# Moving the extra bank half's sum behind the last pair's matmuls, and one factor copy ahead of V0's and V1's copies

## The chip, the cores and the metric

The kernel runs on one core of a Trainium2 chip. The metric is the device time of one execution in microseconds (us). The kernel before was run three times: 461.73, 462.26 and 461.80 us, median 461.80 us.

## What is computed

The reference is a compressed interaction network of three layers over x of shape 1024 x 64 x 16 (batch, feature, embedding):

```python
h = x
for i in range(3):
    z = einsum('bfe,bge->bfge', x, h).reshape(B, 64 * fh, 16)
    y = einsum('oc,bce->boe', W[i], z) + b[i]        # 128 channels
    x_i, h = (y[:, :64], y[:, 64:]) if i < 2 else (y, y)
    xs.append(x_i)
out = sum(concatenate(xs, 1), axis=2) @ fc_w.T + fc_b  # (1024, 1)
```

Everything is float32. The output is one number per batch row, so the part of each layer that goes only into the sum can be folded into weights. The kernel does that: V0 and V1 are such folded weights (`v0`, and `va`/`vb`, made from `in_wx`), and the third layer is folded with `fc_w` into one quadratic form whose matrix lies in `md`.

## The kernel before, in words

**Tiles.** The batch is cut into 32 chunks of 32 rows; a chunk has N = 32 x 16 = 512 columns. For a chunk, `xa` holds the features in four rotations (128 x 4 x 512) and each quarter `xb[j]` holds one further rotation (128 x 512). A product block z is `xa` times one quarter, 128 x 2048, made by VectorE (DVE) or GpSimd (POOL). Before DVE multiplies, ScalarE (ACT) copies the quarter into a PSUM bank (`second`, L550 to L553; the pool tag "y" has two such banks). Sixteen 128-row slices of z against `w_all` give a layer.

**Pairs.** Most chunks go in pairs. A pair's two chunks are multiplied together with fewer matmuls by mixing their z blocks first (`w_mix`, L640 to L652, on POOL: T2 from T3 and X, T3 from T3 and B22, T2 from T2 and B21) and using sums and differences of weights (`ws`). A pair has PSUM banks `alpha`, `delta` and `beta`. Each matmul is 128 rows by 64 columns of weights, so it uses one half of the array's columns and writes one half of a bank; `window` and `zipped` write the matmuls of the two halves alternately into TensorE's (PE's) queue. `squares` then adds terms in x squared and V0 times x (64 x 64 matmuls, four at once).

**Order.** All of this is written by hand: `at(when, fn, ...)` collects steps, and at the end they are emitted in order of `when` (ties in order of collection). So `when` is a place in the queues, not a time. Each engine works through its own queue in that order.

**The first pair (k = 3, chunks 6 and 7).** `make_pair` (L687) emits its copies and products. The product of chunk 6 with quarter 1 is the first pair's X of j = 1; it stands at 26, and its copy `second` at 26 - 2.7 = 23.3. Earlier stand the steps that make V0 and V1: `weigh` on POOL (4 and 5), `add_up` on DVE (17 and 20, L539) and `place` on ACT (17.1 and 20.1, L544). So on ACT the order is: V0's copies, V1's copies, then the copy of chunk 6's quarter 1.

**The end.** The last pair is k = 15. After its window, from t on, two columns are zipped together: the first (one array half) holds three `beta` jobs, two `gamma` jobs (`left_run` with `gamma`), three `delta` jobs and then `end_q` for chunk 3; the second (the other half) holds three `end_q` of chunk 2, seven `alpha` jobs, one `alpha` job with `vb`, and then `end_q` of chunk 2. `gamma` is the half of alpha's bank that alpha leaves free. Its content belongs to alpha's sum: `end_gamma` (L940 to L943), at t + 5, copies it on ACT to the partitions of alpha (L942) and adds it there on DVE into the alpha bank (L943). Chunks 2 and 3 were started at the head of the kernel and end here: `end_squares` at t + 10.5 makes `hx` and `y` (four 64 x 64 matmuls), adds `hx` to the kept `hb` on DVE (L930) and copies two quadrants of it on ACT (L932). `end_pair` emits the last pair's DVE steps: `w_hb` (L665), `w_qa` (L669), `w_ha` (L672), `w_uu` for the second chunk (L675), `x_v0x` (L288, which reads the pair's y bank), and at 13.8 `w_uu` for alpha (L675) and at 14.5 the sum (L292). Then come `x_v0x` and the sum of chunks 2 and 3, `add_parts` (L951), the q sum's second part (34 matmuls of 128 columns), the pooling matmuls (`pools`) and the output.

Of the kernel before, what the change touches and what calls it, by code (L numbers as in the profile page):

```python
# [68 lines left out]
def cin_kernel(ctx, tc, xra, xrb, wh, w0r, w1h, w2t, wx1, wx0, vec, out):  # L69
# [297 lines left out]
    for h in range(2):  # L367
        at = slice(32 * h, 32 * h + 32)
# [145 lines left out]
    def at(when, fn, *args, **flags):  # L514
        ops.append((when, len(ops), fn, args, flags))
# [163 lines left out]
    def make_pair(t, p, when, mixed):  # L679
        a, b = p["a"], p["b"]  # L680
        for when, c, j, name, uses in (
            (when[0], b, 2, "B22", 5), (when[1], b, 0, None, 0), (when[2], b, 0, "T3", 9),
            (when[3], a, 0, "X", 5), (when[4], b, 3, "B22", 6), (when[5], b, 1, None, 0),
            (when[6], b, 1, "T3", 9), (when[7], a, 1, "X", 12 if p["k"] > 3 else 6), (when[8], a, 2, "B21", 5),
            (when[9], a, 3, "B21", 6),
        ):
            if name is None:  # L687
                at(t + when, w_both, p, j)
                continue
            if name == "B21" and j == 2 and p["k"] == 3:  # L690
                at(t + when, w_product, p, c, j, name, uses, engine=nc.gpsimd)
                continue
            if name != "T3":
                at(t + when - (3.3 if p["k"] > 4 and name == "B22" and j == 2 else 2.7), second, c, j)
            at(t + when, w_product, p, c, j, name, uses)
        for when, j, *names in zip(
            mixed, (0, 1, 0, 1, 0, 1), *zip(
                *(2 * (("T2", "T3", "X"),) + 2 * (("T3", "B22", "T2"),) + 2 * (("T2", "T2", "B21"),))
            )
        ):  # L700
            at(t + when, w_mix, p, j, *names)
# [42 lines left out]
    def end_pair(t, p, whens):  # L744
        hb_, qa, uub, ha, uua, xv, add = whens
        at(t + hb_, w_hb, p)
        at(t + qa, w_qa, p)
        at(t + uub, w_uu, p, alpha, "A", snaps[2])
        at(t + ha, w_ha, p)
        at(t + uua, w_uu, p, delta, "O", snaps[0])  # L750
        at(t + xv, x_v0x, p["k"])
        at(t + add, sums, p["k"])
# [80 lines left out]
    for n in range(NPAIR):  # L833
        k = n + 3
        s = k % 2
        p = {
            "k": k, "A": halves[s], "O": halves[1 - s], "b": 2 * k + s, "a": 2 * k + 1 - s,
            "late": 1 + n % 2 if n else 0,
        }
        pairs.append(p)  # L840
        t = T0 + SPAN * n
        if n == 0:
            load_pair(t, p, -39.9, -33.3, -33.15, -27)
            make_pair(
                t, p, (-23.4, -20.7, -20.4, -17.8, -17.2, -16.8, -16.6, -7, -13.5, 3),
                (-14, -6.9, 7.2, 12.4, 16.4, 21.7),
            )
            left5 = [[(contract_half, 5, 3, i, n) for i in (2, 3)] for n in range(2)]
            window(
                t, p, ([left5[1][0], (q_extra, 4, va)], [left5[1][1]]),  # L850
                [left5[0][0], (q_extra, 5, va), None, None], [left5[0][1], None],
                GROUPS,
            )
        else:
            q = pairs[-2]
            load_pair(t, p, -34, -28, -27.8, -27.7)
            make_pair(
                t, p, (-21.4, -18.7, -18.4, -15.8, -12.2, -9.5, -6.1, -2, 1.6, 4.2),
                (-5, 2.8, 7.2, 12.4, 16.4, 21.7),
            )  # L860
            window(t, p, (first_fill(q), second_fill(q)), late_run(q))
            end_pair(t, q, (0.7, 11.7, 17.9, 22.3, 23.2, 24, 27.5))
# [40 lines left out]
    t, q = T0 + SPAN * NPAIR, pairs[-1]  # L903
# [65 lines left out]
    for when, c in ((-5, 2), (0, 3)):  # L969
        at(t + when, product, c, NJ - 1, engine=nc.gpsimd, uses=NI)  # L970
    end_pair(t, q, (0.7, 4.5, 13.8, 8.5, 9, 9.5, 14.5))
    at(t + 5, end_gamma)
    at(t - 0.1, new_ends)
    zipped(
        t,
# [2 lines left out]
        [(end_q, 2, m, 0) for m in range(3)] + late_run(q, False)  # L978
        + [(end_q, 2, m, 0) for m in range(3, NT)] + [(end_extra, 2, 0)],
    )  # L980
    at(t + 10.5, end_squares)
    at(t + 15, x_v0x, 1)
    at(t + 15.1, sums, 1, of=slice(1, 2))
    t += 25
# [98 lines left out]
```

## Time and profile before

| what | value |
|---|---|
| median of three runs | 461.80 us |
| the profiled execution, whole | 462.24 us |
| its span in the trace | 460.4 us |
| PE busy | 453.5 us, 99% |
| DVE busy | 394.0 us, 86% |
| POOL busy | 367.7 us, 80% |
| ACT busy | 117.1 us, 25% |
| TensorE clock granted | 1.00 |

The span is the part that the trace covers; the whole execution has 1.84 us around it. One float32 matmul shows as two records of about 0.59 us. Records of one array half follow one another at 0.43 us (512 columns), the two halves run side by side, and so PE counts as busy as long as one of the halves works. Times within the trace are us from the start of the span. A line of the timeline has start, duration, engine, line of the code, operation, out<-in, how many were merged, and in brackets the idle time before and what ended it.

### The profile page before, as it was taken

The numbers are of one execution on the slowest core, as the hardware profiler recorded it, in microseconds if no ns is written. First come the engines' busy times: TensorE is split into PE (matmuls) and PEld (weight loads), VectorE is DVE, ScalarE is ACT, GpSimd is POOL, SyncE is SP. The second block draws the span as 40 slices with busy tenths as digits, with TensorE's granted clock in tenths as the row PEclk, the third lists the DMA queues.
The fourth block names the chain that finished last, engine by engine and source line by source line (L and its number), as shares of the span: only waits on it lengthen the run. The fifth ranks groups of instructions, "written<-read, shape, count | busy, mean of one in ns | idle before, by whom it ended". The sixth has DMA issues, their size and how long they took to land.

```text
span 460.4 us, 6106 instructions
## 1 busy us (share of the span) xinstructions
PE 453.5 (99%) x2328; PEld 166.5 (36%) x2328; DVE 394.0 (86%) x284; ACT 117.1 (25%) x216; POOL 367.7 (80%) x112
## 2 busy tenths in 40 slices
PE   7999999999999999999999999999999999999997
PEld 4565343343333333333333333333333333333335
DVE  3995599899898989989898998989899998979551
ACT  2162250241313123131213213131311313124011
POOL 5323688998998979899798979989798989989800
DMA  8996998393728173663818264481827448240000
GB/s 295 417 297 149 324 407 321 130 323 111 270 86 319 30 260 140 188 212 131 282 35 290 100 233 166 135 277 48 304 73 250 161 163 279 79 149 18 22 0 2
DMA packets 32613, 86.04 MB, mean 187 GB/s; under 512 B 6116, under 2 KB 6788, under 8 KB 27656
## 3 DMA queue, kind: packets, MB, share of 16 engines
q1 hardware_dynamic: 31800, 84.70, 53.4%
q10 hardware_dynamic: 784, 0.95, 0.8%
q8 instruction: 18, 0.29, 0.3%
q14 instruction: 11, 0.09, 0.1%
HBM read 84.00 MB, written 1.64 MB: 186 GB/s over the span
## 4 chain that ended last, share of the span: by engine, by line
PE 82%; DMA 7%; DVE 3%; SPq 2%; POOL 2%; ACT 1%; issue 1%; POOLq 0%; DVEq 0%
PE alpha L524 57%; PE delta L524 9%; PE beta L524 7%; PE q L524 3%; DMA z<-in_wx 3%; PE acc L250 2%; DMA xa<-in_xra 2%; DVE z L632 2%; DMA xb<-in_xrb 1%; DMA md<-z 1%; SPq L457 1%; POOL z L240 1%; POOL z L535 1%; PE misc L113 1%; PE xp L219 1%
## 5 line engine op out<-in xcount | busy, mean ns | idle before, releaser
L647 POOL TENSOR_TENSOR z<-z,z 128x2048 f32<-128x2048 f32 x78 | 310.4, 4019 | 31.3 <-PE alpha L524 31.3
L632 DVE TENSOR_TENSOR z<-xa,xp 128x2048 f32<-128x2048 f32 x103 | 232.6, 2280 | 16.2 <-POOL z L647 13.1
L524 PE MATMUL alpha<-z,ws 128*64 128x512 f32 x624 | 211.6, 592 | 0.6 <-DVE alpha L943 0.6
L524 PE MATMUL delta<-z,ws 128*64 128x512 f32 x364 | 163.1, 594 | 0.0
L524 PEld LDWEIGHTS alpha<-z,ws 128*64 128x64 f32 x624 | 66.4, 137 | 113.5 <-issue 110.7
L524 PE MATMUL beta<-z,w_all 128*64 128x512 f32 x234 | 105.0, 593 | 0.0
L552 ACT COPY xp<-xb 128x512 f32<-128x512 f32 x88 | 51.6, 588 | 204.8 <-DVE z L632 181.3
L524 PE MATMUL alpha<-z,w_all 128*64 128x512 f32 x208 | 94.2, 595 | 1.1 <-DVE uu L288 0.7
L524 PEld LDWEIGHTS delta<-z,ws 128*64 128x64 f32 x364 | 48.6, 137 | 13.6 <-issue 11.2
L240 DVE TENSOR_TENSOR z<-xa,xp 128x2048 f32<-128x2048 f32 (+2 forms) x23 | 45.1, 2003 | 9.6 <-ACT xp L552 8.2
L524 PEld LDWEIGHTS alpha<-z,w_all 128*64 128x64 f32 x208 | 27.4, 137 | 61.1 <-issue 48.0
L240 POOL TENSOR_TENSOR z<-xa,xb 128x2048 f32<-128x2048 f32 x6 | 27.2, 4557 | 20.6 <-DMA xb<-in_xrb 20.6
L524 PEld LDWEIGHTS beta<-z,w_all 128*64 128x64 f32 x234 | 31.4, 137 | 14.6 <-issue 14.5
L250 PE MATMUL acc<-z,w_all 128*64 128x256 f32 x256 | 29.1, 382 | 1.6 <-DVE z L240 1.4
L524 PE MATMUL acc<-z,w_all 128*64 128x512 f32 (+1 forms) x96 | 30.0, 594 | 0.0
L524 PE MATMUL delta<-z,w_all 128*64 128x512 f32 x52 | 24.6, 593 | 0.0
L250 PEld LDWEIGHTS acc<-z,w_all 128*64 128x64 f32 x256 | 18.0, 137 | 13.8 <-DVE z L240 3.1
L292 DVE TENSOR_REDUCE acc<-uu 128x64 f32<-128x1024 f32 (+2 forms) x19 | 19.6, 1035 | 0.2
L638 DVE TENSOR_TENSOR xp<-xp,xb 128x512 f32<-128x512 f32 x26 | 18.2, 699 | 0.8
L655 ACT COPY snap<-alpha 64x512 f32<-64x512 f32 x13 | 7.6, 581 | 41.7 <-PE delta L524 34.2
L524 PE MATMUL y<-e,v 64*64 64x512 f32 x64 | 17.0, 613 | 0.0
L524 PE MATMUL q<-z,w_all 128*64 128x384 f32 (+1 forms) x128 | 16.9, 381 | 0.0
(117 smaller groups left out, 322.5 us busy)
## 6 DMA issues: line engine op xcount, KB each, us to landing
xa<-in_xra SPq DMA_DIRECT2D x32, 1024.0 KB, 4.7
xb<-in_xrb SPq DMA_DIRECT2D x128, 256.0 KB, 6.8
e<-in_xra SPq DMA_DIRECT2D x28, 128.0 KB, 4.5
xx<-in_xra SPq DMA_DIRECT2D x28, 128.0 KB, 2.5
z<-in_w2t SPq DMA_DIRECT2D x2, 1024.0 KB
z<-in_wx SPq DMA_DIRECT2D x2, 1024.0 KB, 9.2
z<-in_w1h SPq DMA_DIRECT2D x1, 1024.0 KB
xa<-in_xra SPq DMA_DIRECT2D x3, 256.0 KB
```

The source lines that it names most:

```text
L113: nc.tensor.matmul(misc[:, 0:n], zeros, zeros[:, 0:n], start=True, stop=True)
L219: nc.tensor.matmul(xbs[c][j][halves[h]], shift[halves[r], at : at + F], xas[c][halves[r], 0, :], start=True, stop=True,)
L240: engine.tensor_tensor(blocks[zs[c, j]][:, at, :], xas[c][:, at, :], xbs[c][j].unsqueeze(1).to_broadcast([128, last - first, N]), ALU.mult,)
L250: nc.tensor.matmul(accs[c][halves[n]], w_all[:, t, 0:64], blocks[zs[c, j]][:, i, n * H2 : (n + 1) * H2], start=(t == 0), stop=(j == last a ...
L292: nc.vector.tensor_reduce(acc[rows, of, k, half], uu[rows, of if at is None else at, E * half.start : E * half.stop].rearrange("p k (b e) ...
L457: queue.dma_start(out=ms[halves[half], 1, j * NI : (j + 1) * NI], in_=skewed(0, 16 * half + 4 * (j + 1), [[row, NI], [1, F]]),)
L524: nc.tensor.matmul(out, w, rhs, start=start, stop=stop, skip_group_check=True)
L552: nc.scalar.copy(bank, xbs[c][j])
L632: engine.tensor_tensor(blocks[b], xas[c], xbs[c][j].unsqueeze(1).to_broadcast([128, NI, N]), ALU.mult)
L638: nc.vector.tensor_tensor(bank, bank, xbs[p["b"]][j], ALU.add)
L647: nc.gpsimd.tensor_tensor(blocks[o][:, tiles], blocks[x][:, tiles], blocks[y][:, tiles], ALU.subtract)
L655: nc.scalar.copy(snaps[0][p["O"]], alpha(p))
```

## The change

Three places in the emission order are changed. The copy of the first pair's X factor of j = 1 moves from 23.3 to 26 - 9.1 = 16.9, ahead of `place` for V0 (17.1) and V1 (20.1). `end_gamma` moves from t + 5 to t + 11.6. `end_squares` moves from t + 10.5 to t + 10.9. No instruction is added or taken away.

```diff
@@ -691,7 +691,10 @@
                 at(t + when, w_product, p, c, j, name, uses, engine=nc.gpsimd)
                 continue
             if name != "T3":
-                at(t + when - (3.3 if p["k"] > 4 and name == "B22" and j == 2 else 2.7), second, c, j)
+                ahead = 3.3 if p["k"] > 4 and name == "B22" and j == 2 else 2.7
+                if p["k"] == 3 and name == "X" and j == 1:
+                    ahead = 9.1
+                at(t + when - ahead, second, c, j)
             at(t + when, w_product, p, c, j, name, uses)
@@ -969,7 +972,7 @@
     end_pair(t, q, (0.7, 4.5, 13.8, 8.5, 9, 9.5, 14.5))
-    at(t + 5, end_gamma)
+    at(t + 11.6, end_gamma)
     at(t - 0.1, new_ends)
@@ -978,7 +981,7 @@
-    at(t + 10.5, end_squares)
+    at(t + 10.9, end_squares)
     at(t + 15, x_v0x, 1)
```

Seen engine by engine, PE, POOL and the DMA queue keep their order. On ACT the one copy stands ahead of V0's copies instead of behind V1's, and the copy of gamma stands behind the two quadrant copies of L932 instead of ahead of them. On DVE the gamma add stands behind the `hb` add of L930, just ahead of alpha's `w_uu`, instead of ahead of `w_ha`.

## The prediction

> **What bounds the kernel now.** I read the engine shares first (PE 99% of the span), then the chain of waits, then the two stretches that the change touches. PE bounds nearly everywhere, so an edit pays only where PE, or one half of its array, stands. The chain leaves PE in a few places; two are concerned. The first, from the chain in order of time (start us, us, what):
>
> ```profile
> 80.14 2.30 DVE shift L539
> ...
> 83.44 0.60 ACT xp L552
> 84.04 0.02 issue
> 84.07 2.29 DVE z L632
> 86.36 0.67 DVE uu L288
> 87.03 0.04 issue
> 87.07 1.07 PE alpha L524 x2
> ```
>
> V1's reduction, V1's four small copies on ACT (82.46 to 83.43, left out here), the factor copy behind them, the first pair's X product, one more DVE step, and then the first pair's first matmul. The copy waits for nothing but its place in ACT's queue. What stands later in that pair shows in the weight loads of PE, timeline (in brackets the idle time of the load path and what ended it):
>
> ```profile
> 105.01 0.13 PEld L524 LDWEIGHTS delta<-z,ws 128*64 128x64 f32 x1 [0.39 <-POOL z L647]
> ...
> 108.42 0.13 PEld L524 LDWEIGHTS delta<-z,ws 128*64 128x64 f32 x1 [0.37 <-POOL z L647]
> ...
> 112.36 0.13 PEld L524 LDWEIGHTS alpha<-z,w_all 128*64 128x64 f32 x1 [0.99 <-DVE z L632]
> ```
>
> Delta's last seven jobs wait for POOL's mixes, and the next pair's first job waits for DVE. The second stretch is the end. PE timeline:
>
> ```profile
> 432.91 0.59 PE L524 MATMUL alpha<-z,ws 128*64 128x512 f32 x1
> 433.11 0.59 PE L524 MATMUL beta<-e,va 128*64 128x512 f32 x1
> 433.33 2.08 PE L524 MATMUL alpha<-z,ws 128*64 128x512 f32 x7
> 435.26 1.02 PE L524 MATMUL delta<-z,w_all 128*64 128x512 f32 x2
> 436.85 0.64 PE L524 MATMUL alpha<-z,ws 128*64 128x512 f32 x1 [0.57 <-DVE alpha L943]
> ...
> 441.19 1.02 PE L524 MATMUL alpha<-e,vb 128*64 128x512 f32 x2
> 442.14 0.64 PE L524 MATMUL hx<-e,vs 64*64 64x512 f32 x1
> ```
>
> The third alpha job waits for the gamma add on DVE, which waits for the gamma copy on ACT. The idle column says 0.57 us, because one half still works on delta until 436.12; the alpha half has stood since 434.62. DVE's side of it, timeline:
>
> ```profile
> 436.08 0.71 DVE L943 TENSOR_TENSOR alpha<-alpha,snap 64x512 f32<-64x512 f32 x1 [1.66 <-ACT snap L942]
> 438.83 0.69 DVE L672 TENSOR_TENSOR delta<-delta,snap 64x512 f32<-64x512 f32 x1 [2.04 <-PE delta L524]
> 439.56 0.68 DVE L675 SCALAR_TENSOR_TENSOR uu<-delta,snap 64x512 f32<-64x512 f32 x1
> 440.17 0.73 DVE L288 SCALAR_TENSOR_TENSOR uu<-y,cx,xx 128x512 f32<-128x512 f32 x1
> ```
>
> **What the Trainium skill says.** "TensorEngine Tiling (Array Packing)", Key Properties: tiles operate independently, and a change of tiling mode drains TensorE. The trace agrees: the halves carry streams of their own, and the change to 64 x 64 tiles costs 0.09 us (the last alpha slot ends at 441.62 + 0.43 = 442.05, hx starts at 442.14). "TensorE: Matmul & The Clock Gate", Part 3, The mechanism, says matmuls start and end in strict queue order. Across halves this trace differs: the first alpha job (432.91) starts ahead of the gamma job that stands before it in the queue (433.54, when beta's half is free). One unstarted matmul of the other half can be passed; I go by the trace. "Perfetto Trace Analysis", Per-instruction lifecycle, says that waits and the spreading of semaphores lie outside the profiled windows; here that tail is 0.06 us (L943 ends at 436.79, alpha starts at 436.85).
>
> **The change, part by part: the end.** Removed from PE's path: the wait of the third alpha job. ACT's 0.58 us and DVE's 0.71 us are not saved, they move. I lay out both halves from 432.91 with 0.857 us for a 512-column job (two records at 0.43) and 0.645 us for a 384-column q job (two at 0.32).
> - Alpha half: jobs 1 and 2 from 432.91 to 434.62, then six more without a wait: 434.62 + 6 x 0.857 = 439.77.
> - Other half: gamma from 433.54, two gamma and three delta jobs, three q jobs: 433.54 + 5 x 0.857 + 3 x 0.645 = 439.77.
> Both end together, where before the alpha half ended at 442.05: 2.28 us less. Then hx can start at 439.77 + 0.09 = 439.86.
>
> What is late next: the y matmul behind the first hx overwrites the bank that L288 reads. Before, L288 ended at 440.90 and hx started at 442.14, so that wait was covered. Now L672 starts when delta is done. Before, it started 1.07 us after the last delta job's start (437.76 to 438.83); now that job starts at 433.54 + 4 x 0.857 = 436.97, so L672 starts at 438.04, L288 at 439.38, and ends at 440.11. With 0.06 us, y starts at 440.17, 0.30 us after hx. Behind it in PE's queue stand the second hx, the second y and all remaining q matmuls. From the squares to the first q behind them it takes 1.02 us (442.14 to 443.16), so q starts at 440.17 + 1.02 = 441.19 instead of 443.16: **1.97 us**. The bounds: 1.64 if the halves keep strict order (the third alpha job then starts with delta at 435.27 and the half ends at 440.41, so hx and y at 440.50 and q at 441.52), and 2.28 if the y wait costs nothing.
>
> hx itself now carries waits for DVE and ACT of its own: its bank was read last by L669 (ended 434.42) and its input e was made by ACT squares before 424.2, so they cost nothing.
>
> The moved sum: L930 follows hx (second hx about 440.2, its second record ends near 441.3), to 442.0; two quadrant copies on ACT 1.25, to 443.3; gamma copy 0.58, to 443.9; then DVE: add 0.71, L675 0.69, L292 1.22, L288 0.75, L292 0.69, L951 0.72, to about 448.9 with gaps. Before, L951 ended at 448.15. Who waits: the pooling matmuls at 454.30 before, now 452.33, and the q factor step at 452.54 before, now 450.6. About 3.4 and 1.7 us of cover. All the rest, to the output, follows PE and moves with it.
>
> **The first pair.** The copy waits for DVE (the bank's last reader, X of j = 0, done at 72.0) and for its quarter's DMA, issued at 63.52 or soon after, in a stretch whose DMA share falls from 1.03 (72 to 76) to 0.57 (76 to 80) and 0.04 (80 to 84). So it lands by about 78.3, while ACT idles from 71.70 to 79.59: V0's copies are not held. The X product follows the reduction directly: 82.45 instead of 84.07, 1.62 us. The L288 steps end at 85.35 and 86.05. PE's last job before ends at 84.47 + 4 x 0.43 = 86.19, so alpha starts at about 86.22 instead of 87.07 and delta at 86.25 instead of 87.73: 0.85 and 1.48 us.
>
> What is late next: POOL. From 75.55 (the second weigh, which waits for V1's load) to 112.88 its instructions follow each other without a gap: 4.56 + 4.54 + 4.54 + 23.81 = 37.45 us. Nothing of that starts earlier. Its mix for delta ends at 104.93, delta starts at 105.01 whatever came before, runs 14 records to 111.08, and the squares start at 111.17 as before. The gain is lost there. What stays: the next pair's first alpha waits for its X product, which ended at 112.32. DVE comes about 0.85 us earlier (its copies follow PE through L655 and L658), so PE can start at 111.17 + 1.02 = 112.19 instead of 112.36: **0.17 us**, which the following windows, bound by PE, carry on. Bounds: 0, and 0.85 if POOL didn't hold (1.48 at most, delta's shift).
>
> **Sum.** 1.97 + 0.17 = 2.14 us: the profiled execution, 462.24 us (span 460.4 and 1.84 around it), becomes 460.10. It lies 0.44 above the median of 461.80, from which I forecast 461.80 - 2.14 = 459.66, **459.7 us**.
>
> **The rivals.**
> - Strict order of the halves: 1.64 + 0.17 = 1.81, 460.0 us. For: the skill's page. Against: 432.91 ahead of 433.54.
> - The first pair's gain goes through, because POOL's hold is weaker than it looks: 1.97 + 0.85 to 1.48, 458.4 to 459.0 us. For: the chain names ACT and DVE there. Against: the two waits on POOL at 105.01 and 108.42.
> - Only the idle time that PE's column shows comes back, because the halves' lag doesn't close: 0.57 + 0.17, 461.1 us, no measurable change. Against: the rows from 440.66 to 442.05 hold alpha alone, one half standing, which is what the first half's wait cost.
> - Slower: the moved sum becomes the end's bound. Place: PE's first pooling matmul waits for L951, and all later q matmuls stand behind it. It decides once the chain from 441.3 to 448.9 grows by over 3.4 us, and is slower than before from 5.5. If that chain of 7.6 us took twice as long, 4.2 us would be lost: 459.7 + 4.2 = 463.9 us. For: nine dependent steps over two engines. Against: each has its measured duration.
>
> **How the numbers follow.** The forecast has 0.68 (459.2 to 460.2), strict order 0.12, gain through 0.10, idle only 0.07, slower 0.03. About 0.2% (0.9 us) is what a measurement of this kernel can tell from no change. Faster: 0.68 + 0.12 + 0.10 = 0.90; same 0.07; slower 0.03. A range from 458.8 to 460.8 leaves out "idle only", "slower" and most of "gain through", about 0.17.
>
> **What would show it.** Right: in the last stretch alpha and delta or q records pair up without a hole after 434.62, hx starts near 439.9, y about 0.3 after it, the q run near 441.2; L951 ends ahead of the pooling matmuls. At the first pair: alpha near 86.2, delta's wait on POOL still at 105.01 and longer than 0.39, the next window at about 112.2. Wrong: the squares start ahead of 111, a DMA wait in front of the moved copy, or V0's copies after 79.6.

## The result and the profile after

The changed kernel took 458.90 us (median of four runs, 458.56 to 460.21) against 462.03 us (four runs, 461.73 to 462.45): ratio 0.9937, interval 0.9915 to 0.9958, so 1.9 to 3.9 us less. Its profiled execution took 458.84 us with a span of 457.0 us, 3.4 us less than the span of before. The forecast was 2.14 us less. The ratios and intervals use the fast executions alone: one of the last version below was slow (465.26 us at a granted clock of 0.993) and is left out there.

The end first. The stretch from the first beta job to the first q job behind the squares, PE timeline of the kernel before:

```profile
430.91 0.64 PE L524 MATMUL beta<-z,w_all 128*64 128x512 f32 x1
...
443.16 8.61 PE L524 MATMUL q<-z,w_all 128*64 128x384 f32 x52
```

PE timeline of the kernel after:

```profile
429.81 0.64 PE L524 MATMUL beta<-z,w_all 128*64 128x512 f32 x1
...
431.80 0.59 PE L524 MATMUL alpha<-z,ws 128*64 128x512 f32 x1
432.01 0.59 PE L524 MATMUL beta<-e,va 128*64 128x512 f32 x1
432.23 2.31 PE L524 MATMUL alpha<-z,ws 128*64 128x512 f32 x9
434.15 0.59 PE L524 MATMUL delta<-z,w_all 128*64 128x512 f32 x1
434.38 0.59 PE L524 MATMUL alpha<-z,ws 128*64 128x512 f32 x1
...
438.24 0.59 PE L524 MATMUL alpha<-e,vb 128*64 128x512 f32 x1
438.34 0.49 PE L524 MATMUL q<-z,w_all 128*64 128x384 f32 x1
438.76 0.64 PE L524 MATMUL hx<-e,vs 64*64 64x512 f32 x1
439.10 0.61 PE L524 MATMUL y<-e,v 64*64 64x512 f32 x1
...
440.11 8.61 PE L524 MATMUL q<-z,w_all 128*64 128x384 f32 x52
```

The merged row ahead of delta's first record has nine records and not seven. Four of them are gamma's, which lie in alpha's bank; the two more are the third alpha job, which passed the delta job that stands before it in the queue. From there alpha and delta, then alpha and q records interleave, and both halves end together (438.24 + 0.43 = 438.67 and 438.34 + 0.32 = 438.66). y starts 0.34 us behind hx. The whole stretch takes 429.81 to 440.11 = 10.30 us; before it was 430.91 to 443.16 = 12.25. That is **1.95 us**.

DVE timeline after, the same stretch:

```profile
436.93 0.69 DVE L672 TENSOR_TENSOR delta<-delta,snap 64x512 f32<-64x512 f32 x1 [3.61 <-PE delta L524]
437.65 0.68 DVE L675 SCALAR_TENSOR_TENSOR uu<-delta,snap 64x512 f32<-64x512 f32 x1
438.26 0.73 DVE L288 SCALAR_TENSOR_TENSOR uu<-y,cx,xx 128x512 f32<-128x512 f32 x1
440.22 0.69 DVE L933 TENSOR_TENSOR hb<-hx,hb 128x512 f32<-128x512 f32 x1 [1.22 <-PE y L524]
442.82 0.71 DVE L946 TENSOR_TENSOR alpha<-alpha,snap 64x512 f32<-64x512 f32 x1 [1.91 <-ACT snap L945]
...
446.99 0.72 DVE L954 TENSOR_TENSOR acc<-acc 128x32 f32<-128x32 f32 x2
449.41 0.56 DVE L939 SCALAR_TENSOR_TENSOR uu<-q,snap 128x384 f32<-128x384 f32 x1 [1.70 <-PE q L524]
```

(L933, L939, L946 and L954 are L930, L936, L943 and L951 of before.) L288 ends at 438.99 and y starts at 439.10, so it seems that DVE now releases it; the y bank below tests that. The moved sum ends at 447.71; the pooling matmuls start at 451.25, 3.54 us later, and L939 still waits 1.70 us for PE: the sum is covered.

The first pair. PE weight loads before, at the squares (the next window's first load, 112.36, stands in the prediction):

```profile
111.16 0.13 PEld L524 LDWEIGHTS alpha<-e,vs 64*64 64x64 f32 x1 [0.81 <-issue]
```

PE weight loads after:

```profile
104.09 0.13 PEld L524 LDWEIGHTS delta<-z,ws 128*64 128x64 f32 x1 [0.83 <-POOL z L647]
...
110.24 0.13 PEld L524 LDWEIGHTS alpha<-e,vs 64*64 64x64 f32 x1 [0.81 <-issue]
...
111.26 0.13 PEld L524 LDWEIGHTS alpha<-z,w_all 128*64 128x64 f32 x1 [0.81 <-DVE z L632]
```

Alpha and delta start together at 85.76 and 85.77, without a wait. Delta's later wait on POOL has grown from 0.39 to 0.83 us: PE comes earlier and waits longer. From the squares to the second pair's window it takes 1.02 us instead of 1.19 to 1.20: **0.17 us**. But the window itself comes 1.10 us earlier than before (111.26 and 112.36). The rest lies ahead of the change's reach. POOL timeline, the second weighing, before and after:

```profile
75.55 4.56 POOL L535 TENSOR_TENSOR z<-z,vs 128x2048 f32<-128x2048 f32 x1 [0.44 <-DMA z<-in_wx]
```

```profile
74.58 4.58 POOL L535 TENSOR_TENSOR z<-z,vs 128x2048 f32<-128x2048 f32 x1 [0.74 <-DMA z<-in_wx]
```

By its bracket this step waits for V1's load; it starts 0.97 us earlier, and from there to the squares it takes the same 35.6 to 35.7 us. The last part lies behind the last output's issue, before and after:

```profile
457.97 0.24 SPq L1011 DMA_DIRECT2D out<-hb  x1
```

```profile
454.92 0.25 SPq L1014 DMA_DIRECT2D out<-hb  x1
```

To the end of the span (460.4 and 457.0, given to 0.1 us) it takes 2.43 and 2.08 us, 0.35 less. So 0.97 + 0.17 + 1.95 + 0.35 = 3.44 makes up the span's 3.40, the difference being rounding and the 0.04 in POOL's stretch. Two of the four terms were forecast. Do the other two belong to the change?

### The profile page after: what moved, and what is told of

It is laid out like the page before. It is cut to its first block, busy times and chain, and to the rows that moved or that the text cites. A ratio compares the mean times of both kernels' runs of the same rounds, so it can differ in the third digit from the quotient of the medians.

```text
span 457.0 us, 6105 instructions
## 1 busy us (share of the span) xinstructions
PE 451.5 (99%) x2328; PEld 163.8 (36%) x2328; DVE 393.6 (86%) x284; ACT 117.0 (26%) x216; POOL 367.8 (80%) x112
## 4 chain that ended last, share of the span: by engine, by line
PE 97%; DMA 2%; SPq 0%; issue 0%; DVE 0%; ACT 0%; ACTq 0%
PE alpha L524 59%; PE delta L524 10%; PE beta L524 7%; PE acc L524 6%; PE acc L250 6%; PE q L524 3%; PE acc L268 3%; DMA z<-in_w0r 2%; PE y L524 1%; PE pm L384 0%; PE pv L357 0%; SPq L144 0%; PE xp L219 0%; PE hx L524 0%; PE pc L892 0%
## 5 line engine op out<-in xcount | busy, mean ns | idle before, releaser
L524 PE MATMUL q<-z,w_all 128*64 128x384 f32 (+1 forms) x128 | 16.9, 381 | 0.0
```

Source lines behind the costliest of these rows:

```text
L524: nc.tensor.matmul(out, w, rhs, start=start, stop=stop, skip_group_check=True)
```

## The experiments

Theory A: the end is worth its 1.95 us, the copy 0.17 because POOL holds the first pair, and the landing of V0's and V1's loads differs from execution to execution. Theory B: the copy is worth the 1.1 us by which the window came earlier. Two whole times of one kernel differ by 1 us and more, so the verdicts rest on distances within a trace: from the second weighing's start to the squares and to the second pair's window for the first pair, from beta to q for the end. In kernels that agree in the stretch these repeat to 0.07 us or better.

**The parts alone.** The changed kernel with the copy put back:

```diff
-                if p["k"] == 3 and name == "X" and j == 1:
-                    ahead = 9.1
```

> Only the end's moves (gamma's copy and add behind the squares); the first factor copy stays behind V1's copies. Theory A (the end is worth what its queues say, the rest of the measured gain is how V1's load happened to land): from the last pair's first beta job to the first q behind the squares 10.30 us as in the changed kernel, against 12.25 before, so 1.95 us less than before, about 460.1 us. Theory B (the copy is worth the 1.1 us by which the second pair's window came earlier): the same 1.95 here. Strict order of the halves: 10.6 us in that stretch, 1.64 less.

Beta to q: 429.97 to 440.27 = 10.30 us. Squares to window: 110.21 to 111.42 = 1.21, as before. Ratio 0.9936 (0.9913 to 0.9958). The whole 1.95 belongs to the end's moves, and the forecast's passing of halves holds without the copy.

The copy alone (the end of before):

```diff
-    at(t + 11.6, end_gamma)
+    at(t + 5, end_gamma)
...
-    at(t + 10.9, end_squares)
+    at(t + 10.5, end_squares)
```

> Only the first factor copy ahead of V0's and V1's copies; the end as before. Theory A: POOL holds delta's last seven jobs, so only the gap from the squares to the second pair's first alpha closes, from 1.19 to 1.02 us: 0.17 us less than before, about 461.9 us; the time from POOL's second weighing (L535) to the squares stays at 35.6 us (before 75.55 to 111.17, after 74.58 to 110.24). Theory B: about 1.1 us less than before, 460.9 us, and that time shrinks.

Beta to q: 430.24 to 442.49 = 12.25, as before. PE weight loads of this kernel:

```profile
104.52 0.13 PEld L524 LDWEIGHTS delta<-z,ws 128*64 128x64 f32 x1 [1.26 <-POOL z L647]
...
110.67 0.13 PEld L524 LDWEIGHTS alpha<-e,vs 64*64 64x64 f32 x1 [0.81 <-issue]
...
111.69 0.13 PEld L524 LDWEIGHTS alpha<-z,w_all 128*64 128x64 f32 x1 [0.81 <-DVE z L632]
```

The second weighing started at 74.99: 35.68 us to the squares, 1.02 to the window. Ratio 0.9998 (0.9986 to 1.0010), so at most 0.65 us of gain: theory B's 1.1 is excluded. DVE's product for this window was done at 106.41 + 4.49 = 110.90, 35.91 us after the weighing instead of 112.32 - 75.55 = 36.77: it came 0.86 us earlier, and the forecast had 0.85. PE started at 111.69, so DVE, which the last bracket still names, was 0.8 us ahead of what held the window.

That `end_squares` stands at 10.9 instead of 10.5 does nothing: no step lies between the two places, and with 10.5 the changed kernel is the same program.

**The same kernel again.**

> The changed kernel once more, for how far two executions of one kernel differ in the start of POOL's second weighing (74.58 us in its first trace, 75.55 in the one of before) and in the tail from the last reduction to the end of the span. Theory A: the start of the weighing moves by up to 1 us between executions, and the second pair's window moves with it one to one, 36.68 us later. Theory B: it stays near 74.6 in kernels with the moved copy and near 75.5 in those without.

POOL and PE weight loads of this execution:

```profile
75.30 4.55 POOL L535 TENSOR_TENSOR z<-z,vs 128x2048 f32<-128x2048 f32 x1 [0.31 <-DMA z<-in_wx]
```

```profile
110.97 0.13 PEld L524 LDWEIGHTS alpha<-e,vs 64*64 64x64 f32 x1 [0.81 <-issue]
...
111.99 0.13 PEld L524 LDWEIGHTS alpha<-z,w_all 128*64 128x64 f32 x1 [0.81 <-DVE z L632]
```

The same kernel, but the weighing starts 0.72 us later than in its first trace, the window 0.73 us later, and the span is 0.8 us longer. Beta to q is 10.30 again. Ratio 0.9963 (0.9943 to 0.9983): 0.8 to 2.6 us less than before. Over all eleven traces the weighing started between 74.15 and 76.08 us, both kinds of kernel mixed. In four of them it follows the first weighing without a gap, so that V0's load, which the first one waits for, sets its start, and not V1's. Theory A.

**Is it POOL that holds?** Two kernels, one with the copy's move and one without, both with the old end, leave out three of the four slices of one POOL product ahead of its mixes (B21 of j = 2; their output is not the reference's, only their time is of use):

```diff
-                at(t + when, w_product, p, c, j, name, uses, engine=nc.gpsimd)
+                at(t + when, w_product, p, c, j, name, uses, engine=nc.gpsimd, last=1)
...
-            blocks[b], xas[c], xbs[c][j].unsqueeze(1).to_broadcast([128, NI, N]), ALU.mult
+            blocks[b][:, 0:last], xas[c][:, 0:last],
+            xbs[c][j].unsqueeze(1).to_broadcast([128, last, N]), ALU.mult
```

> Leaves out three of the four slices of one product of the first pair (B21 of j = 2, on POOL), which takes about 3.4 us from POOL's queue ahead of its mixes; with the moved copy, the end as before. Theory A (POOL's hold hides the copy's gain): delta's wait on POOL ends about 1.5 to 2.5 us earlier after the second weighing's start, and the second pair's window starts about 0.7 us earlier after that start than with the moved copy alone (36.66 us), near 36.0, where DVE's product or PE itself comes next. If POOL doesn't bound, 36.66 as with the copy alone.

> The same slices left out, without the moved copy; the end as before. Theory A: delta starts earlier, but the second pair's first alpha job still waits for DVE's product, which the unmoved copy holds back: the window starts 36.8 us after the second weighing's start, as before (36.81), so taking work from POOL is worth nothing without the copy's move. If POOL were the only bound, about 1 us less.

PE weight loads with the moved copy, then without it:

```profile
109.02 0.13 PEld L524 LDWEIGHTS alpha<-e,vs 64*64 64x64 f32 x1 [0.81 <-issue]
...
111.42 0.13 PEld L524 LDWEIGHTS alpha<-z,w_all 128*64 128x64 f32 x1 [2.19 <-DVE z L632]
```

```profile
110.13 0.13 PEld L524 LDWEIGHTS alpha<-e,vs 64*64 64x64 f32 x1 [0.81 <-issue]
...
112.29 0.13 PEld L524 LDWEIGHTS alpha<-z,w_all 128*64 128x64 f32 x1 [1.95 <-DVE z L632]
```

The weighings started at 76.08 and 75.47. With the move: squares after 32.94 us, window after 35.34. Without: 34.66 and 36.82. So with POOL relieved the move is worth 1.48 us by these distances, and 0.87 in plain times (112.29 to 111.42). The distance says too much: V1 landed 0.61 us later in the first kernel, and its first alpha job, at 86.23, already followed PE's own last job, which doesn't move with V1. Either way it is several times what the copy alone gives by the same distance, 0.13 us (36.81 and 36.82 without the move, 36.68 to 36.70 with it). And relieving POOL is worth nothing without the move: 36.82. Each of two waits hid the other: the window waits for POOL's way and for DVE's. I had expected 36.0 with both, and it was 35.34. No wait of delta on POOL is left in that kernel, so delta's half gains too; that DVE's earlier product comes from this is argued and not shown. Whole times: 0.9986 (0.9973 to 0.9999) and 1.0003 (0.9993 to 1.0012).

The other way round, work put into POOL's queue of the changed kernel:

```diff
+    def pad_step():
+        nc.gpsimd.tensor_tensor(uu[:, 1, :].rearrange("p (k c) -> p k c", c=F), ws[:, 1], ws[:, 2], ALU.subtract)
+
+    at(5.5, pad_step)
```

> The changed kernel with one needless POOL subtraction of 128 x 512 (about 1.3 us) right behind the second weighing. Theory A: POOL runs without a gap from there to delta's last seven jobs, so the squares come 1.3 us later after the weighing's start (36.95 instead of 35.65) and the whole is 1.3 us longer. If POOL had room, no change.

The needless step took 1.28 us. Weighing at 74.15, squares at 111.04: 36.89 us instead of 35.66, so 1.23 us later; the weight load that ends delta's first wait on POOL came at 104.89, 30.74 us after the weighing instead of 104.09 - 74.58 = 29.51. Ratio to the kernel before 0.9976 (0.9965 to 0.9988), about 1.1 us less than it, where the changed kernel was 1.7 and 2.9 less. POOL's chain passes on 1.23 of the 1.28 us.

**The wait that took the removed one's place.** y in a bank that nobody reads any more:

```diff
-            v0x(c, "set")
+            v0x(c, "y")
```

> The changed kernel with chunks 2 and 3's y in one of the two banks of the factor copies, which nobody reads any more, so that its matmul doesn't wait for the last pair's L288. Theory A: y starts with the first hx instead of 0.34 us after it, and from hx to q it takes 1.02 us instead of 1.35: 0.33 us less than the changed kernel. If the wait were covered by something else (the mode change, the load of weights), nothing.

PE timeline:

```profile
438.93 0.64 PE L524 MATMUL hx<-e,vs 64*64 64x512 f32 x1
438.93 0.64 PE L524 MATMUL y<-e,v 64*64 64x512 f32 x1
...
439.95 6.35 PE L524 MATMUL q<-z,w_all 128*64 128x384 f32 x38
```

hx to q takes 1.02 us again, beta to q 429.97 to 439.95 = 9.98, 0.32 less than the changed kernel. Ratio 0.9936 (0.9912 to 0.9960). The whole times don't separate it from the changed kernel; the stretch does.

**The 0.35 us behind the last output.** One needless copy on ACT, early:

```diff
+    def one_more():
+        nc.scalar.copy(fv2[:, 0:1], vs[:, 0:1])
+
+    at(3.2, one_more)
```

> The changed kernel with one needless one-column copy on ACT early on. From the issue of the last output to the end of the span it takes 2.43 and 2.51 us in the two kernels with the old end and 2.08 to 2.15 in the four with the new one; the new end has one waiting instruction less on ACT and one less on DVE, and one packet less in an instruction queue (10 instead of 11). If ACT's count decides, this copy brings back 11 packets and about 2.45 us; if DVE's or neither, it stays at 10 and 2.1.

DMA queue part of the page, this kernel and the changed kernel:

```profile
q14 instruction: 11, 0.09, 0.0%
```

```profile
q14 instruction: 10, 0.08, 0.1%
```

Eleven packets, and 454.92 to 457.4 = 2.48 us from the last output's issue to the end (one execution), where the changed kernel had 2.08. In the traces, waiting instructions included, ACT has 322 instructions in the kernel before and 321 after the change, whose gamma copy waits for one engine instead of two; DVE has 404 and 403. The kernel with the needless POOL step has DVE's 404 back, but ACT's 321: ten packets and 2.08 us. So ACT's count decides. All five traces with 322 gave 11 packets and 2.41 to 2.51 us, all six with 321 gave 10 and 2.08 to 2.15. Why a packet more of instructions makes the end longer isn't shown.

**A version made from this.** The y bank above, and one slice of that B21 product made by DVE while it waits for the weighing:

```diff
-                at(t + when, w_product, p, c, j, name, uses, engine=nc.gpsimd)
+                at(t + when, w_product, p, c, j, name, uses, engine=nc.gpsimd, first=1)
+                at(t + when, w_slice, p, c, j, name)
...
+    def w_slice(p, c, j, name):
+        nc.vector.tensor_tensor(blocks[p[name][j % 2]][:, 0], xas[c][:, 0], xbs[c][j], ALU.mult)
```

> The changed kernel with the y bank of the run above, and one of the four slices of the first pair's B21 product of j = 2 made by DVE, where it waits for the second weighing, instead of POOL; the same result. Theory A: POOL's chain from the second weighing to delta's last seven jobs gets about 1.1 us shorter (3.4 instead of 4.54 us for the product), DVE's path is 1.3 us ahead of POOL's and gives away up to 0.7, so the second pair's window starts 35.5 to 36.0 us after the weighing's start (36.66 before that) and from beta to q it takes 9.98 us: 0.33 + 0.7 to 1.1 less than the changed kernel, about 457.9 us. If POOL's chain were not what holds, 36.66.

POOL timeline:

```profile
74.78 4.57 POOL L535 TENSOR_TENSOR z<-z,vs 128x2048 f32<-128x2048 f32 x1 [0.29 <-DVE xp L642]
79.31 5.05 POOL L651 TENSOR_TENSOR z<-z,z 128x2048 f32<-128x2048 f32 x1
84.32 3.47 POOL L632 TENSOR_TENSOR z<-xa,xb 128x1536 f32<-128x1536 f32 x1
```

The product got 1.07 us shorter, but the mix ahead of it, beside which DVE made its slice (79.26 to 79.94), took 5.05 instead of 4.55 us. The squares came 35.06 us after the weighing (35.66 in the changed kernel), and the window after 36.31, because PE now waits for DVE, whose product ended at 106.55 + 4.49 = 111.04 (window 111.09). Beta to q: 9.97. By the distances it gains 0.37 + 0.33 us over the changed kernel, its span of 456.5 us is the shortest; but its whole times run from 457.95 to 465.26 us (22 executions, median 459.16), ratio 0.9973 (0.9951 to 0.9996), and that it beats the changed kernel is not shown. The long executions go with a lower granted clock: the fourteen at 1.000 took 457.95 to 461.30 us, median 458.51, the eight at 0.993 to 0.996 took 460.27 to 465.26. The kernel before, measured beside it, had three of 27 at such a clock (462.80 to 463.77 us). What lowers the clock, and whether this version does it more often, stays open. Of the versions run, the y bank alone is the one to keep, by its stretch of 9.98 us.

## Why the prediction was right

The direction, the range and both mechanisms held.

- **The alpha half.** Forecast: both halves end together, 2.28 us earlier, and hx starts at once. Measured in the beta-to-q frame: hx came 442.14 - 430.91 = 11.23 us after beta before, 8.95 after, 2.28 less. The strict-order rival fell: the third alpha job passed delta's. With it fell, for starts in two column halves, what the Trainium skill says ("TensorE: Matmul & The Clock Gate", Part 3, The mechanism: matmuls start and end in strict queue order). So a place in PE's queue is not always the order of starts.
- **The y wait.** Forecast 0.30 us, measured 0.34; 0.32 when taken away. Together 1.97 forecast, 1.95 measured.
- **The moved sum.** Cover forecast 3.4 and 1.7 us, measured 3.54 and 1.70. The slower rival's place exists, but it is far away.
- **The first pair.** Alpha and delta started together, as the sum had it. POOL's hold forecast from a gapless queue: shown from both sides, by taking work out and putting it in. Forecast 0.17, measured 0.17 to 0.19 from the squares to the window and 0.13 from the weighing to the window. The rival that let the gain through (0.85 to 1.48) would have been right with some 3.2 us less on POOL (4.54 to 1.30 for the one product).
- **Idle time only.** The rival with 0.57 us fell: the column of idle time showed a quarter of what the half lost.

The signs of being wrong were badly chosen, since they stand in times from the start of the span. All three came true to the letter, and none for the reason meant: the squares started ahead of 111 (110.24, from the earlier weighing), V0's copies after 79.6 (79.73, released by DVE's reduction; the moved copy had ended at 75.74), and in the repeat a DMA wait of 4.28 us stood in front of the moved copy (75.88), in ACT's idle time. Of the times named for being right there, 86.2, 105.01 and 112.2, none was met either (85.76, 104.09 and 111.26). What decides are the distances.

What the sum missed: 0.35 us at the very end, since I looked only at who waits. The change does alter the number of instructions: in their new places the steps need one waiting instruction less on ACT, one less on DVE and one more on PE (6106 in the trace before, 6105 after). With the end's 0.35 the change is worth 1.95 + 0.17 + 0.35 = 2.47 us, inside the intervals of both measurements of the changed kernel (1.9 to 3.9 and 0.8 to 2.6). The other 0.97 us in the first pair of traces is the landing of a load, and not the change: the distances show that. In part the first number was lucky: 458.90 lies 0.8 us below the forecast and just inside its range, and the repeat of the same kernel, 459.88, lies 0.2 above it.

## What to carry to other kernels

Where two column halves of TensorE carry streams of their own, lay out each half by itself: a wait that shows as 0.57 us of idle TensorE cost one half 2.28 us, and a place behind the squares, where 3.54 us of other work cover it, made it free. Before a gain is booked at one wait, follow the pair to where its ways meet again: here POOL's gapless queue left 0.13 to 0.17 us of a gain of 0.87 to 1.48. And when two traces differ, take distances from the last common event; the start of a load-bound step alone differed by up to 1.9 us between executions.

## What the runs showed of the hardware

- A matmul can pass an unstarted one of the other column half (alpha's third job ahead of delta's first, which stands before it in the queue: 433.52, in steps of 0.43 from 431.80, against 434.15).
- One instruction more on ACT (322 instead of 321 in the trace; tried with one early copy, and seen with one waiting instruction) went with one packet more in an instruction queue and some 0.3 to 0.4 us more behind the last output (2.41 to 2.51 against 2.08 to 2.15).
- In one trace, a POOL mix beside a 128 x 512 product of 0.68 us on DVE with both inputs in SBUF was 0.50 us longer (5.05 and 4.55). The Trainium skill names such a contention ("GPSIMD Engine Reference", section 1, Specifications: the SBUF interfaces are shared with VectorE, and its instructions with two SBUF inputs contend); this run agrees with it.
